# Two graph attention layers: own rows taken from gathered tiles, and the order of sums and turns in layer 1

## The chip, the cores and the metric

The kernel runs on one core of a Trainium2 chip. The metric is the device time of one execution in microseconds (us). The engines are PE (TensorE: matmuls, transposes), DVE (VectorE), ACT (ScalarE), POOL (GpSimd) and SP (SyncE, here only for DMAs). DMAs are issued by SP, ACT and POOL; the indirect ones, which gather or scatter rows by a list of row numbers, by POOL.

## The reference

There are 2708 nodes with 1024 features each, and an adjacency matrix in which a node has its own edge and about 16 others. Each layer is an attention over the neighbours, then a residual sum and a layer norm:

```python
def _L0_gnn_ref(x, adj, Wf, bf, Wg, bg, W, bW):
    e = jax.nn.relu((x @ Wf + bf) @ (x @ Wg + bg).T)
    scores = jnp.where(adj > 0, e, NEG)
    return jax.nn.softmax(scores, axis=1) @ (x @ W + bW)

def _L1_gnn_ref(x, adj, W, a1, a2):
    h = x @ W
    e = jax.nn.leaky_relu(h @ a1 + (h @ a2).T, negative_slope=0.2)
    scores = jnp.where(adj > 0, e, NEG)
    return jax.nn.relu(jax.nn.softmax(scores, axis=1) @ h)

x = _layernorm(x + _L0_gnn_ref(x, adj, ...), axis=-1)
x = _layernorm(x + _L1_gnn_ref(x, adj, ...), axis=-1)
```

## The kernel before

**Lists (lines 189 to 515).** In place of dense attention, the kernel turns each row of `adj` into a list of at most 40 neighbours. For each of 22 blocks of 128 rows, `lists(b)` (line 405) loads 128 x 2708 integers, makes them 0 or 1 on ACT with a row sum (410), multiplies them on POOL with `iota` (412), which holds 8192 minus the column, and takes the largest values on DVE: 8 from each of 20 segments (415), then 40 from those in five rounds (419). A larger value is a smaller column, so a list `L` holds its columns in rising order, with zeros behind the last. `keep_lists` (430) makes column numbers of it on ACT, 8192 for an unused place, and writes them to `LD` in device memory. These are ordered by the scheduler of the language. In between, PE forms `M = Wf Wg^T` and other small products, with copies on ACT and a few row operations on POOL (`row_parts`, 255). A node's number of neighbours gives its class; the nodes are sorted by class, and every 32 of the sorted nodes are a group: 85 groups with 3 to 10 tiles, 405 in all. Four groups are a block; block 0 has one group with 20 valid rows.

**A tile** is 128 gathered rows: partition 32q + i holds the neighbour at place 4t + q of the list of the group's node i, t being the tile's number in the group. So place 0 of all lists of a group lies in partitions 0 to 31 of its tile t = 0.

**Order of work.** From line 520 on all five engines are used through `InOrder` (line 61): instructions of one engine keep the order in which the program issues them. Each engine's queue is thus written by hand, and a waiting instruction holds up all behind it on its engine.

**Layer 0 (lines 868 to 1105)** gathers rows of `x` into a ring of 20 slots; per tile DVE forms 128 dot products (line 886), PE sums the rows with the softmax weights, turns the sums, and multiplies with `W`. `close(b)` (932) adds the residual, normalises, writes the rows to `X1S` by SP (948), forms two dot products (950, 951) and scatters the rows by POOL with their score to `T1`, from which layer 1 gathers.

**Layer 1 (lines 1108 to 1262).** `z = x1[done1[b] % 3]` names one of three buffers, `rb`, `u1b`, `u2b`. A ring of 33 slots (`ring` and `more`) holds gathered rows of `T1`, 4112 bytes each. The blocks run in the order of their sums of tiles. A block with four groups has two parts, `ks` = (0, 1) and (2, 3); block 0 has one; that makes 43 parts of 3 to 14 tiles. For each part the loop at line 1215 issues:

1. `lay.sums` (815): PE, two matmuls (both halves of the 1024 columns) per tile, into the bank `po`.
2. The rest of `closing`: POOL scatters a finished block to `out` (1171).
3. `lay.gathers(latest)` (669): POOL gathers into the slots that this part has freed, the slot freed last first.
4. One `piece` (1201), if one is there: the product of half a block with `M`, which now holds the layer's `W`, eight matmuls on PE.
5. `turn_half` (1207) of the part before: four transposes on PE; with a block's last part, its two halves are put into `pieces`.
6. `scores1` of the next part (1137): DVE adds and softmax weights, with one exponential on ACT (796).
7. `lay.out` (839): ACT writes `y`, the sums divided by their totals.
8. The copies of the turned part to `yT` on ACT.
9. After a block's last part, `mark_over` (1176) for two more blocks: POOL sets a mark in `over` for each tile that a group doesn't use, one memset per group; once, `count_over` (1185) compares the marks with the lists on DVE, PE and ACT.
10. If a block's second half product has just been issued, `close1` (1157): SP loads the block's rows of `X1S` into `z`, DVE adds relu of the product and computes mean and variance, ACT normalises.

Behind the loop the remaining half products and the last block follow (1249 to 1261).

The score of a gathered row lies at column 1024 of its slot. `unfit` (101, 1245) sends inputs that don't fit the lists to another path, which these inputs don't take.

Of the kernel before, what the change touches and what calls it, by code (L numbers as in the profile page):

```python
# [8 lines left out]
F32 = mybir.dt.float32  # L9
BF16 = mybir.dt.bfloat16  # L10
I32 = mybir.dt.int32
AF = mybir.ActivationFunctionType
ALU = mybir.AluOpType
# [22 lines left out]
NONE = 8192  # L36
# [21 lines left out]
TILES = [SORTED[_g] for _g in GROUPS]  # L58
# [48 lines left out]
def listed_path(ctx, tc, x, adj, Wf, bf, Wg, bg, W, bW, W1, a1, a2, out):  # L107

    nc = tc.nc
    P = 128  # L110
    N, D = x.shape
    KC = D // P
    H = D // 512
    TW = D + 4
    NB = (N + P - 1) // P
# [4 lines left out]
    valid = [N - 32 * (NG - 1)] + [P] * (NB - 1)  # L120
    start = [0] + [valid[0] + P * b for b in range(NB - 1)]
# [19 lines left out]

    LD = dram.tile([N * Q, QT], I32, name="LD")
    T1 = dram.tile([N, TW], F32, name="T1")
    X1S = dram.tile([N, D], F32, name="X1S")

    ident = const.tile([P, P], F32, name="ident")
    make_identity(nc, ident)
# [49 lines left out]
    with tc.tile_pool(name="pre", bufs=1) as pre:  # L197
# [8 lines left out]
        for t in (tot, cnt, cls):  # L206
            nc.vector.memset(t, -1.0)
        nc.vector.memset(L[:, NB - 1, :], 0.0)
        none = pre.tile([P, 1], F32, name="none")
        nc.gpsimd.memset(none, float(NONE))  # L210

        def ramp(name, count, step, base, dtype=F32, part=0):
            t = pre.tile([P, count], dtype, name=name)
            nc.gpsimd.iota(t, pattern=[[step, count]], base=base, channel_multiplier=part,
                           allow_small_or_imprecise_dtypes=True)
            return t

        fours = ramp("fours", QT, 4, 0)
        classes = ramp("classes", NCL, 1, 0)
        lows = ramp("lows", 32, 1, 0)  # L220
# [31 lines left out]
        with tc.tile_pool(name="adjp", bufs=3) as adjp, tc.tile_pool(name="cands", bufs=2) as cands, \  # L252
# [152 lines left out]
            def lists(b):  # L405
                n = nsize[b]
                t = adjp.tile([P, N], I32, name="adj")
                sp.dma_start(t[:n], adj[b * P:b * P + n, :])
                k = t.bitcast(F32)
                act.activation(k[:n], t[:n], AF.Relu, accum_out=tot[:n, b:b + 1])  # L410
                for cut in ([slice(0, 10 * SEG), slice(10 * SEG, N)] if b == 0 else [slice(0, N)]):
                    nc.gpsimd.tensor_tensor(k[:n, cut], k[:n, cut], iota[:n, cut], op=ALU.mult)  # L412
                cand = cands.tile([P, NSEG, 8], F32, name="cand")
                for s in range(NSEG):
                    nc.vector.max(cand[:n, s, :], k[:n, s * SEG:min((s + 1) * SEG, N)])  # L415
                flat = cand.rearrange("p s e -> p (s e)")
                for r in range(CAP // 8):
                    top = L[:n, b, r * 8:(r + 1) * 8]
                    nc.vector.max(top, flat[:n])
                    if r + 1 < CAP // 8:  # L420
                        nc.vector.match_replace(flat[:n], top, flat[:n], 0.0)
                j2 = cands.tile([P, CAP], F32, name="j2")
                nc.vector.tensor_scalar(j2[:n], L[:n, b, :], 0.0, 0.0, op0=ALU.is_gt, op1=ALU.add,
                                        accum_out=cnt[:n, b:b + 1])

                j3 = cands.tile([P, QT], F32, name="j3")
                nc.vector.tensor_scalar(j3[:n], fours[:n], cnt[:n, b:b + 1], 0.0, op0=ALU.is_lt, op1=ALU.add,
                                        accum_out=cls[:n, b:b + 1])

            def keep_lists(b):  # L430
                n = nsize[b]
                act.activation(PL[:n, b], L[:n, b].rearrange("p (t q) -> p q t", q=Q), AF.Relu,
                                     scale=-1.0, bias=none[:n])
                act.dma_start(LD.rearrange("(n q) t -> n (q t)", q=Q)[b * P:b * P + n, :],
                                    PL[:n, b].rearrange("p q t -> p (q t)"))

# [65 lines left out]
        for q in range(Q):  # L502
# [8 lines left out]
        t = pre.tile([P, NB], F32, name="badu")  # L511
        nc.vector.tensor_scalar(t, cnt, 0.0, 0.0, op0=ALU.is_equal, op1=ALU.add, accum_out=bad[:, 2:3])
        t = pre.tile([P, NB], F32, name="badv")
        nc.vector.tensor_scalar(t, L[:, :, 0], float(NONE), 0.0, op0=ALU.is_gt, op1=ALU.add,
                                accum_out=bad[:, 3:4])


# [351 lines left out]
    with ExitStack() as s0s:  # L869
# [62 lines left out]
        def close(b):  # L932

            n, m, z = nrows[b], valid[b], Z.pop(b)
            pm = Wp.pop(b)

            def add(h):
                c = slice(h * 512, (h + 1) * 512)
                dve.tensor_add(z[:n, c], pm[h][:n, h, :], z[:n, c])

            if b + 1 < NB:
                dve.tensor_add(z[:n, :D], flat(pm)[:n], z[:n, :D])
            steps = norm(z, n, None if b + 1 < NB else add)
            next(steps)
            yield
            for _ in steps:
                pass
            sp.dma_start(X1S[start[b]:start[b] + m, :], z[:m, :D])
            yield
            dot(z[:n, :D], u2b, n, z[:n, D:D + 1])  # L950
            dot(z[:n, :D], u1b, n, f1[:n, b:b + 1])
            yield
            if z is not zs:
                pool.memset(z[:, D + 1:], 0.0)
            scatter(T1[:, :], ids[:m, b:b + 1], z[:m])
# [152 lines left out]
    with ExitStack() as s1s:  # L1108
# [28 lines left out]
        def scores1(u, ks):  # L1137
# [16 lines left out]
            dve.tensor_add(sc, sc, off)  # L1154
            lay.soft(u, ks)

        def close1(b, pm):
            m, z = valid[b], x1[done1[b] % 3]
            sp.dma_start(z[:m], X1S[start[b]:start[b] + m, :])
            last = b == order1[-1]  # L1160

            def add(h):
                c = slice(h * 512, (h + 1) * 512)
                dve.scalar_tensor_tensor(z[:m, c], pm[h][:m, h, :], 0.0, z[:m, c], op0=ALU.max, op1=ALU.add)

            if not last:
                dve.scalar_tensor_tensor(z[:m], flat(pm)[:m], 0.0, z[:m], op0=ALU.max, op1=ALU.add)
            for _ in norm(z, m, add if last else None):
                pass
            yield  # L1170
            scatter(out, ids[:m, b:b + 1], z[:m])
# [4 lines left out]
        def mark_over(b):  # L1176

            for g in groups[b]:
                if g == 0:
                    for q in range(Q):  # L1180
                        pool.memset(over[32 * q:32 * q + valid[0], 0, TILES[0]:], 1.0)
                elif TILES[g] < QT:
                    pool.memset(over[:, g, TILES[g]:], 1.0)

        def count_over():
            dve.scalar_tensor_tensor(over, SL, float(N), over, op0=ALU.is_lt, op1=ALU.mult)
# [5 lines left out]

        parts = [(u, ks) for u in units for ks in (((0, 1), (2, 3)) if u.G == Q else ((0,),))]
        lay.gathers()
        pool.memset(over, 0.0)
        scores1(*parts[0])
        closing, pieces, turning = iter(()), [], None
        banks = ps_s.tile([P, H, 512], F32, name="po")
        yT = {}

        def piece(b, h, pm):
            if h == 0:
                pm.append(ps_m.tile([P, H, 512], F32, name="pm"))
            half_product(pm[0], h, nrows[b], yT[b], M)
            return (b, pm[0]) if h + 1 == H else None

        def turn_half(u, ks, y):
            b = u.b
            if ks[0] == 0:
                yT[b] = tp.tile([P, KC, P], F32, name="yT")  # L1210
            steps = lay.turn(y, ks, yT[b])
            next(steps)
            return steps

        for n, (u, ks) in enumerate(parts):
            b, po = u.b, banks[:, n % 2, :]
            latest = lay.sums(u, po, ks)
            for _ in closing:
                pass
            closing = iter(())  # L1220
            lay.gathers(latest)
            made = pieces.pop(0)() if pieces else None
            steps = iter(())
            if turning is not None:
                v, kv, _ = turning
                steps = turn_half(*turning)
                if kv[-1] + 1 == v.G:
                    pm = []
                    pieces += [lambda c=v.b, h=h, pm=pm: piece(c, h, pm) for h in range(H)]
            if n + 1 < len(parts):  # L1230
                scores1(*parts[n + 1])
            y = yp.tile([P, 512], F32, name="y1")
            lay.out(u, po, ks, y)
            for _ in steps:
                pass
            turning = u, ks, y
            if ks[-1] + 1 == u.G:
                k = done1[b]
                for i in (2 * k, 2 * k + 1):
                    if i < NB:  # L1240
                        mark_over(i)
                if k == NB // 2 + 1:
                    count_over()
                if k + 2 == NB:
                    unfit = nc.values_load(flag[0:1, 0:1])
            if made is not None:
                closing = close1(*made)
                next(closing)
        while pieces:
            made = pieces.pop(0)()  # L1250
        for _ in turn_half(*turning):
            pass
        for _ in closing:
            pass
        closing = close1(*made)
        next(closing)
        prod = two_products(P, yT[b], M)
        for _ in closing:
            pass
# [366 lines left out]
```

## Time and profile before

| | |
|---|---|
| median of 3 executions | 1890.39 us (1887.95 to 1898.44) |
| the profiled execution | 1750.29 us, span 1748.6 us |
| mean clock granted to PE | 0.957 |
| busy: PE, DVE, ACT, POOL | 1563.6, 1297.5, 643.5, 1180.9 us |
| moved by DMA | 502.8 MB, mean 288 GB/s |
| read from and written to device memory | 509.6 MB, 33.8 MB |
| gathers in layer 0, layer 1 | 405, 249 + 156 |
| transfers of `X1S`: written, read | 22, 22 (512 KB each for a full block) |

The span is the time from the first to the last instruction of the profiled execution. In views by time, columns are the start and the length in us, the engine, the line, the operation and the tiles that it writes and reads; a bracket behind gives the idle time of the engine just before, and what ended it. Since nearly all engine calls of the two layers pass through `InOrder`, they carry its line, L71; the names of the tiles tell them apart: `po` are the weighted sums, `pm` the products, `pt` the turned data. `ring<-in_x_dram,SL` is a gather of layer 0, `ring<-T,SL` and `more<-T,SL` are gathers of layer 1. "issue" is time in which an engine waited for nothing that the profile shows.

### The profile page before, as it was taken

How to read it: one execution, taken by the hardware profiler on the slowest of the kernel's cores; microseconds unless marked ns; L12 is line 12 of the kernel's file. 1: busy time of each engine (PE TensorE's matmuls, PEld its weight loads, DVE VectorE, ACT ScalarE, POOL GpSimd, SP SyncE). 2: the span in 40 equal slices, each digit the busy share in tenths (PEclk: the TensorE clock that was granted, in tenths of full speed). 3: DMA queues.
4: the chain of work that ended last, by engine and by line, in shares of the span. 5: the costliest groups of instructions: out<-in, count | busy, mean ns of one | idle time of the engine just before them, and what ended most of it. 6: DMA issues, size and time to landing. Idle time of an engine off the chain costs nothing. (4 is left out here: it accounts for less than half of the span.)

```text
span 1748.6 us, 23112 instructions
## 1 busy us (share of the span) xinstructions
PE 1563.6 (89%) x6969; PEld 675.5 (39%) x6969; DVE 1297.5 (74%) x4262; ACT 643.5 (37%) x902; POOL 1180.9 (68%) x1195
## 2 busy tenths in 40 slices
PE   4999578899999999999999999559899888999896
PEld 2444233344444444444444444213344333343332
DVE  5879846899999989998999977547465555665652
ACT  4555455444444554555554444101111111111111
POOL 7888476467667767776677743177777777777740
PEclk8999778999999999999999999879999999999998
DMA  7656168578877777888887876399999999999960
GB/s 287 228 185 236 38 232 309 199 252 292 302 277 283 269 253 276 294 293 284 303 299 285 291 267 249 121 394 357 367 374 392 391 397 375 384 392 390 396 253 38
DMA packets 149986, 502.80 MB, mean 288 GB/s; under 512 B 32340, under 2 KB 32372, under 8 KB 147144
## 3 DMA queue, kind: packets, MB, share of 16 engines
q0 software_dynamic: 132032, 428.29, 66.2%
q1 hardware_dynamic: 10202, 55.72, 8.4%
q10 hardware_dynamic: 7618, 17.23, 2.7%
q8 instruction: 57, 0.93, 0.2%
q14 instruction: 77, 0.63, 0.1%
HBM read 509.64 MB, written 33.75 MB: 311 GB/s over the span
## 5 line engine op out<-in xcount | busy, mean ns | idle before, releaser
L71 POOL DMA_INDIRECT ring<-in_x_dram,SL x405 | 429.9, 1062 | 164.0 <-issue 70.0
L71 DVE SCALAR_TENSOR_TENSOR j<-ring,Fr 128x1024 bf16<-128x1024 f32 x402 | 493.9, 1229 | 41.1 <-DMA ring<-in_x_dram,SL 13.9
L71 PE MATMUL po<-ring,st 128*32 128x512 f32 x2616 | 324.4, 616 | 56.9 <-ACT y L71 32.5
L71 ACT COPY Fr<-pm 32x1024 f32<-32x1024 f32 (+2 forms) x353 | 340.6, 965 | 18.8 <-PE pm L71 14.1
L71 PE MATMUL pm<-M,yT 128*128 128x512 f32 (+1 forms) x704 | 313.3, 598 | 0.5 <-ACT yT L71 0.5
L71 PE MATMUL pm<-Wt,xT 128*128 128x512 f32 (+1 forms) x704 | 300.5, 599 | 4.7 <-DMA Wt<-in_L_gnn_W_dram 4.7
L71 POOL DMA_INDIRECT ring<-T,SL x249 | 247.0, 992 | 80.5 <-issue 66.3
L71 PE MATMUL pm<-M,xT 128*128 128x512 f32 x672 | 297.5, 601 | 0.0
L71 ACT ACTIVATE scores<-scores 128x12 f32<-128x12 f32 (+9 forms) x65 | 14.0, 216 | 631.6 <-DVE scores L71 631.6
L71 PEld LDWEIGHTS pm<-M,yT 128*128 128x128 f32 (+1 forms) x704 | 127.8, 186 | 185.0 <-issue 183.8
L71 PEld LDWEIGHTS pm<-Wt,xT 128*128 128x128 f32 (+1 forms) x704 | 131.0, 189 | 163.4 <-issue 154.6
L71 PEld LDWEIGHTS pm<-M,xT 128*128 128x128 f32 x672 | 130.2, 194 | 158.0 <-issue 155.1
L71 POOL DMA_INDIRECT more<-T,SL x156 | 154.6, 991 | 48.5 <-issue 43.8
L71 PEld LDWEIGHTS po<-ring,st 128*32 128x32 f32 x2616 | 95.9, 113 | 229.8 <-issue 174.0
L412 POOL TENSOR_TENSOR adj<-adj,iota 128x2708 f32<-128x2708 f32 (+3 forms) x23 | 130.6, 5685 | 22.7 <-ACT adj L71 22.6
L415 DVE MAX8 cand<-adj 128x8 f32<-128x136 f32 (+2 forms) x440 | 97.2, 285 | 37.4 <-POOL adj L412 37.4
L71 PE MATMUL pm<-halfT,WfT 128*128 128x512 f32 x256 | 114.1, 601 | 1.1 <-ACT WfT L71 1.1
L71 POOL DMA_INDIRECT SL<-LD,idq x85 | 86.4, 1016 | 25.8 <-issue 24.0
L71 PE MATMUL po<-more,st 128*32 128x512 f32 x624 | 82.4, 625 | 14.3 <-ACT y L71 14.3
L71 DVE TENSOR_SCALAR scores<-ring,f1q 128x4 f32<-128x4 f32 (+6 forms) x69 | 16.5, 245 | 104.1 <-DMA ring<-T,SL 93.1
L71 POOL DMA_INDIRECT z<-in_x_dram,ids x21 | 24.0, 1142 | 87.1 <-DVE j L71 36.4
L71 PEld LDWEIGHTS pm<-halfT,WfT 128*128 128x128 f32 x256 | 48.2, 193 | 58.0 <-issue 55.2
(214 smaller groups left out, 1539.5 us busy)
## 6 DMA issues: line engine op xcount, KB each, us to landing
adj<-in_adj_dram SPq DMA_DIRECT2D x21, 1354.0 KB, 5.8
X1S<-z SPq DMA_DIRECT2D x19, 512.0 KB, 5.2
ring<-in_x_dram,SL POOLq DMA_INDIRECT x405, 6.5
rows<-in_L_gnn_Wg_dram ACTq DMA_DIRECT2D x8, 512.0 KB, 4.4
rows<-in_L_gnn_Wf_dram ACTq DMA_DIRECT2D x8, 512.0 KB, 3.5
rows<-in_L_gnn_W_dram ACTq DMA_DIRECT2D x8, 512.0 KB, 6.1
Wt<-in_L_gnn_W_dram ACTq DMA_DIRECT2D x1, 4096.0 KB
M<-in_L_gnn_W_dram SPq DMA_DIRECT2D x1, 4096.0 KB
```

The source lines that it names most:

```text
L71: made = self.tc.keep_in_program_order(op(*args, **kwargs))
L412: nc.gpsimd.tensor_tensor(k[:n, cut], k[:n, cut], iota[:n, cut], op=ALU.mult)
L415: nc.vector.max(cand[:n, s, :], k[:n, s * SEG:min((s + 1) * SEG, N)])
```

## The change

The own key of each row is doubled on POOL, so that it is the largest of its list and comes to place 0; ACT halves it again when the column numbers are made. The rows of `X1S` are then the rows 0 to 31 of the tiles with t = 0, which layer 1 gathers in any case. `X1S` goes, with its writes in layer 0 and its loads in layer 1. `own_rows` copies the rows from the ring to `z` on ACT, one copy of 32 x 1024 per group, behind the copies of the turned part in the loop. `y` and the turning now belong to the same part: `lay.out` is issued ahead of the half product, `turn_half` behind it, and the scores of the next part after both. The half products of a block so start one part earlier, and the steps behind the loop that finished the last turn and one half product go. `mark_over` and the clearing of `over` are issued on DVE. The test on the first place of a list compares the other way.

```diff
-    X1S = dram.tile([N, D], F32, name="X1S")
...
+        nc.vector.memset(L[:, NB - 1, 0:1], 4.0 * NONE)
...
+        twice = SL.rearrange("p g t -> p (g t)").bitcast(F32)[:, :P]
+        nc.gpsimd.tensor_scalar(twice, ident, 1.0, None, op0=ALU.add)
...
+                own = slice(b * P, b * P + n)
+                nc.gpsimd.tensor_tensor(k[:n, own], k[:n, own], twice[:n, :n], op=ALU.mult)
...
+                act.activation(PL[:n, b, 0, 0:1], L[:n, b, 0:1], AF.Relu, scale=-0.5, bias=none[:n])
...
-        nc.vector.tensor_scalar(t, L[:, :, 0], float(NONE), 0.0, op0=ALU.is_gt, op1=ALU.add,
+        nc.vector.tensor_scalar(t, L[:, :, 0], float(NONE), 0.0, op0=ALU.is_le, op1=ALU.add,
...
-            sp.dma_start(X1S[start[b]:start[b] + m, :], z[:m, :D])
...
+        def own_rows(u, ks):
+
+            z = x1[done1[u.b] % 3]
+            for k in ks:
+                m = next(i for i, tile in enumerate(u.tiles) if tile[0] == k)
+                n = min(32, valid[u.b])
+                act.copy(z[32 * k:32 * k + n], lay.rows(u.at + m)[:n, :D])
+
         def close1(b, pm):
             m, z = valid[b], x1[done1[b] % 3]
-            sp.dma_start(z[:m], X1S[start[b]:start[b] + m, :])
...
-                        pool.memset(over[32 * q:32 * q + valid[0], 0, TILES[0]:], 1.0)
+                        dve.memset(over[32 * q:32 * q + valid[0], 0, TILES[0]:], 1.0)
                 elif TILES[g] < QT:
-                    pool.memset(over[:, g, TILES[g]:], 1.0)
+                    dve.memset(over[:, g, TILES[g]:], 1.0)
...
-        pool.memset(over, 0.0)
+        dve.memset(over, 0.0)
         scores1(*parts[0])
-        closing, pieces, turning = iter(()), [], None
+        own_rows(*parts[0])
+        closing, pieces = iter(()), []
...
             lay.gathers(latest)
+            y = yp.tile([P, 512], F32, name="y1")
+            lay.out(u, po, ks, y)
             made = pieces.pop(0)() if pieces else None
-            steps = iter(())
-            if turning is not None:
-                v, kv, _ = turning
-                steps = turn_half(*turning)
-                if kv[-1] + 1 == v.G:
-                    pm = []
-                    pieces += [lambda c=v.b, h=h, pm=pm: piece(c, h, pm) for h in range(H)]
+            steps = turn_half(u, ks, y)
+            if ks[-1] + 1 == u.G:
+                pm = []
+                pieces += [lambda c=b, h=h, pm=pm: piece(c, h, pm) for h in range(H)]
             if n + 1 < len(parts):
                 scores1(*parts[n + 1])
-            y = yp.tile([P, 512], F32, name="y1")
-            lay.out(u, po, ks, y)
             for _ in steps:
                 pass
-            turning = u, ks, y
+            if n + 1 < len(parts):
+                own_rows(*parts[n + 1])
...
-        while pieces:
-            made = pieces.pop(0)()
-        for _ in turn_half(*turning):
-            pass
-        for _ in closing:
-            pass
-        closing = close1(*made)
-        next(closing)
         prod = two_products(P, yT[b], M)
```

## The prediction, made before the result was known

> **What bounds the kernel now.** I read three views in this order: the busy tenths of the whole span (page, part 2), the busy times by stage over layer 1, and the order in time of single engines where layer 1 begins, runs and ends.
>
> ```profile
> PE   4999578899999999999999999559899888999896
> DVE  5879846899999989998999977547465555665652
> POOL 7888476467667767776677743177777777777740
> DMA  7656168578877777888887876399999999999960
> ```
>
> Slices are 43.7 us. Slices 1 to 5 make the lists, up to slice 25 is layer 0 (PE and DVE full, POOL and DMA not), slices 27 to 39 are layer 1. There the DMA engines stand at 9, PE near 9 and POOL at a steady 7. The steady 7 is the important one:
>
> ```profile
> 1300.00:1400.00 100.00, 90.67 (x441) 39.82 (x439) 58.77 (x286) 14.75 (x34) 77.29 (x101) 0.98 1.01 388
> 1500.00:1600.00 100.00, 96.12 (x470) 39.85 (x463) 59.18 (x282) 14.89 (x32) 76.53 (x78) 0.98 1.01 391
> ```
>
> Columns: PE, PE loads, DVE, ACT, POOL busy, clock, DMA share, GB/s. Looked at instruction by instruction, POOL's 77 is a full queue:
>
> ```profile
> 1219.91 0.99 POOL L71 DMA_INDIRECT more<-T,SL  x1 [0.30 <-issue]
> 1221.20 0.99 POOL L71 DMA_INDIRECT more<-T,SL  x1 [0.30 <-issue]
> 1222.18 0.37 POOL L71 MEMSET over<- 128x3 f32 x8
> 1222.70 1.00 POOL L71 DMA_INDIRECT ring<-T,SL  x1 [0.15 <-issue]
> ...
> 1664.44 1.01 POOL L71 DMA_INDIRECT ring<-T,SL  x1 [0.30 <-issue]
> 1667.46 0.99 POOL L71 DMA_INDIRECT more<-T,SL  x1 [2.02 <-issue]
> ```
>
> Each gather occupies POOL for 0.99 + 0.30 = 1.295 us, back to back. From the first gather at 1133.72 to the last at 1686.89, 553.2 us, there are 404 steps: 404 x 1.295 = 523.2, 18 scatters of `out` x 1.31 = 23.6, and what is left, 6.4 us, is memsets and a few stalls. The same 1.295 stands at the start, when the DMA engines have just become busy, and the waits of POOL between 1200 and 1640 are almost only "issue" of 0.3. So layer 1 is paced by POOL's issuing, with the DMA engines (share 1.0) and PE close behind: a block of 20 tiles costs POOL 20 x 1.295 + 1.5 = 27.4 us and PE 24.2 (sums 5.45 + 3.64, two half products of 7.13, two turns of 0.43).
>
> After the last gather PE sets the end:
>
> ```profile
> 1700.56 4.03 PE L71 MATMUL po<-ring,st 128*32 128x512 f32 x34
> 1704.52 7.13 PE L71 MATMUL pm<-M,yT 128*128 128x512 f32 x16
> 1711.49 0.60 PE L71 MATMUL pt<-ident,y 128*128 128x128 f32 x4
> 1711.92 7.03 PE L71 MATMUL pm<-M,yT 128*128 128x512 f32 x16
> 1718.79 0.60 PE L71 MATMUL pt<-ident,y 128*128 128x128 f32 x4
> 1719.86 14.00 PE L71 MATMUL pm<-M,yT 128*128 128x512 f32 x32 [0.46 <-ACT yT L71]
> ```
>
> Last sums, a half product, a turn, the block's other half product, the last turn, the last block's product: two half products lie between the last sums and the last product.
>
> [...] gathers landed 6.2 us after issue at the start of layer 1 (1136.37 to 1142.56) and up to 10.3 later, beside reloads of X1S and scatters. [...] the trace has 5.94 us for 2708, 2.19 ns. [...] the trace's scaled pass over 128x1024 in SBUF is 1.24, its 32x1024 copies out of PSUM 1.0. [...] here the clock is 0.97 to 1.0 wherever PE is busy.
>
> **The change part by part.**
>
> *X1S is no longer written (22 SP transfers).* These lie in layer 0, where PE (97%) and DVE (92%) are full and DMA is at 0.67 to 0.84. DVE waited 13 us for gathers in all of it. I take 0; bounds -3 and 0.
>
> *X1S is no longer read (22 transfers, 11.1 MB).* At 388 GB/s this is 28.6 us of DMA time, but POOL's pace doesn't follow from DMA time. Three places do. (a) At the seam:
>
> ```profile
> 1127.05 1.33 POOL L71 DMA_INDIRECT T<-ring,ids  x1 [14.05 <-DVE j L71]
> 1133.72 1.03 POOL L71 DMA_INDIRECT ring<-T,SL  x1 [5.33 <-DMA T<-ring,ids]
> ```
>
> The first gather waits for the last scatter, 5.87 us, with three 512 KB transfers of X1S and one of 80 KB started from 1125.0 to 1128.8. The DMA view has a median of 3.7 for the two scatters of this kind, and 3.4 for the fastest of all. I take -2.2 (bounds -2.5, 0). (b) The gather at 1667.46 stalled 1.7 us beyond 0.3, three before it 0.3 together, where landings took 10 us. I take half of 2.0: -1.0 (-2.0, 0). (c) Landing of the last but one part, whose last gather went out at 1675.23 and whose scores were complete at 1683.1: 7.9 us against 6.2 undisturbed. I take -0.8 (-1.7, 0).
>
> *Own rows on ACT: 85 copies at 1.1 us* [...], 2.2 us per part. ACT is busy 15 of 100 us in layer 1, so I take 0. The wait counts more: the first copies of a block overwrite the buffer whose `out` scatter belongs to three blocks before. Behind them on ACT stand the normalised rows of another block, the next `y`, then the next exponential, for which PE and DVE wait. Putting each scatter just ahead of the gathers that follow it in the new order, and 7.5 us for its landing, it lands 11 and 9 us after ACT asks for it in two early blocks, and from 2.8 late to 4.2 early in the others. About 9 us of lateness are covered (3.6 to 5.4 of sums and 7.1 of half product on PE, less ACT's own 3). So PE loses some 2 us early, where POOL is 18 to 20 us behind the slots that PE has freed: hidden. Without that cover it would be 2 us.
>
> *Sums turned at once.* Per part nothing is added. On ACT the exponential now follows `y`; `y` waits for the sums just ended and has the half product (7.1) as cover. One half product moves from the tail into the second part of layer 1, where PE waited 3.4 us for data, so PE runs some 3.5 us later from there; slots are freed at least 5.3 us ahead of the gather that takes them, so POOL doesn't see it. In the tail one of the two half products and a turn gap go: 1704.52 to 1719.86 is 15.3, afterwards 7.1 + 0.43 + 0.5: **-7.3** (-8, -5). One more scatter (1.31 us) stands before the last 7 gathers; the last part's sums waited for PE and not for data (exponential at 1694.5, sums at 1700.1), so 0.
>
> *Marks on VectorE.* On POOL go: the clearing (1176.27 to the next gather 0.98, less 0.30), the first eight marks (1.39 less 0.30) and ten groups of eight at 0.22 beyond the usual gap, as at 1222.18: 0.7 + 1.1 + 2.1 = **-3.9** (-4.2, -3). On DVE eight memsets at 0.08 per block, 0.7 us, where it is busy 59%; the clearing falls into its wait of 13 us for the first gather: 0.
>
> *Own key first.* Per block POOL gets a 128x128 product: 128 x 2.19 = 0.28, with a gap 0.34. It counts where DVE waits for POOL:
>
> ```profile
> 136.10 0.30 DVE L415 MAX8 cand<-adj 128x8 f32<-128x136 f32 x1 [1.69 <-POOL adj L412]
> 197.85 1.30 DVE L415 MAX8 cand<-adj 20x8 f32<-20x136 f32 x6 [0.26 <-POOL adj L412]
> ```
>
> Up to 136.1 POOL runs from 111.72 with three blocks: 3 x 0.34. From there DVE works without a gap to 197.85, where POOL is again just in time, with two more on its side: 5 x 0.34 = **+1.7** (+1, +2.8). `twice` (about 0.3) is under POOL's wait of 0.5 for the first mask. A one-column ACT pass per block (0.16 to 0.2) is under ACT's waits of 3.6 us per step for PE. Comparing the other way costs nothing.
>
> **Sum:** -2.2 - 1.0 - 0.8 - 7.3 - 3.9 + 1.7 = **-13.5**, so the profiled execution of 1750.3 (span 1748.6) becomes 1736.8, a ratio of 0.9923. The shown runs have a median of 1890.4, 140 us more, and the profile doesn't say where those lie; I carry the ratio over: 1875.9, written **1876**.
>
> **The rivals.**
> *PE paces the runs.* If the 140 us are slower matmuls, PE's 24.2 us per block reach POOL's 27.4, and what POOL saves is worth nothing; a half product that only moves saves the 3.4 us of early idle less 2 for ACT's wait. With -2.2 + 1.7 this is about -2: 1888. For it: PE is near full in both layers. Against it: the clock in the trace [...].
> *DMA time paces the runs.* If the 140 us are slower transfers, the bytes count: -28.6 - 2.2 - 7.3 + 1.7 = -36, 1851. For it: share 1.0. Against it: 1.295 at any load.
> *The copies stall ACT (slower).* If scatters land later than I place them, for instance 13 us after ACT's need in all 19 full blocks, PE loses 13 - 9 = 4 per block, 3.2 of them within POOL's margin; at 15 us it is 2.8 beyond the margin, 19 x 2.8 = 53 less 13.5 gained: about 1930; it turns into a loss against the present from 12.9. For it: the two early blocks. Against it: in the rest the order in time leaves it near 0.
> *An unseen wait at the gathers* (85 of them now also follow an ACT copy) at a sixth of the 0.30 gap each, a guess, gives back 4: 1880.
>
> **How the numbers follow.** Forecast 0.47, with the unseen wait 0.1; PE 0.22; DMA 0.1; ACT stall or another loss 0.11. Within the forecast its bounds give 1869 to 1883. 0.5% (9.5 us, about what a measurement of this kernel can tell from no change) puts the line at 1881. Faster: 0.43 of the forecast, 0.06, and DMA's 0.1, less a little: 0.57; within 0.5%: 0.31; slower 0.12. The range takes in PE's case and half of DMA's: 1859 to 1892.
>
> **What would show it.** Right: no transfer of X1S; POOL from first to last gather 548 us or less, still at 1.295; one half product between the last sums and the last product; first gather 2 us sooner after the last scatter; lists ending 1 to 3 us later. Wrong: ACT copies with idle time released by `out`; POOL waiting for PE or ACT; a gather step other than 1.295 with DMA below 1.

## The result, and the profile after

The changed kernel took **1956.13 us** (median of 4 executions, 1947.51 to 1960.44), against 1891.87 for the kernel before in the same set of runs (4 executions, 1887.95 to 1898.44): a ratio of **1.0387** (95% interval 1.0326 to 1.0448). Forecast were 1876 and 0.9923. The change made this measurement slower by 3.9%.

The same program differed by up to 9% between sets of runs: the kernel before had medians of 1892, 1903, 1897 and 1905 us in four sets and of 1748, 1749 and 1750 in three. So all ratios here are within one set. They leave out executions that stand more than 1.5% above the fastest of their kernel; where I count executions, all of them are counted.

The page of the changed kernel, 40 slices of 49 us. Added to the rows that were shown of before is the clock granted to PE:

```profile
PE   5999468688888889899999989469978887978886
DVE  5979447778767777688888868426635454555543
POOL 8988444555555555566676752366664666666640
PEclk9999679788888989899999999769988998999988
DMA  6745346656666666667777775399886999999960
```

Layer 0 is slices 5 to 26. In slices 9 to 16 (counted from 1) DVE has fallen from 8 or 9 to between 6 and 8, POOL from 6 or 7 to 5, DMA from 7 or 8 to 6 (5 in one), and the clock stands at 7 to 9. After that the slices of layer 0 come back towards those of before. The stretch in numbers, and two stretches of layer 1 (columns as in the windows of before: PE, PE loads, DVE, ACT, POOL busy, clock, DMA share, GB/s):

```profile
430.00:880.00 450.00, 398.15 (x1665) 169.54 (x1665) 338.16 (x753) 190.87 (x228) 254.74 (x244) 0.90 0.63 222
880.00:1090.00 210.00, 201.41 (x902) 89.14 (x901) 184.56 (x407) 103.78 (x125) 145.06 (x134) 1.00 0.76 261
1300.00:1400.00 100.00, 92.29 (x404) 32.94 (x406) 57.74 (x320) 31.62 (x51) 65.28 (x67) 0.92 0.89 311
1500.00:1600.00 100.00, 86.53 (x376) 33.84 (x380) 49.93 (x255) 27.09 (x43) 62.28 (x63) 0.90 0.86 307
```

The first row has 1665 matmuls in 450 us at a mean clock of 0.90. In layer 1 POOL has fallen from 77 to between 62 and 65, with DMA below 0.9: POOL's queue no longer paces it. An instant from layer 1 shows what does (all engines in order of time):

```profile
1705.04 1.03 PE L71 MATMUL po<-ring,st 128*32 128x512 f32 x4
...
1705.99 7.13 PE L71 MATMUL pm<-M,yT 128*128 128x512 f32 x16
...
1706.73 0.17 DVE L71 TENSOR_TENSOR scores<-scores,mq 128x10 f32<-128x10 f32 x1
...
1716.16 0.69 ACT L71 ACTIVATE y<-po,ri 128x512 f32<-128x512 f32 x1 [11.77 <-remote]
1716.34 0.99 POOL L71 DMA_INDIRECT ring<-T,SL  x1 [2.03 <-remote]
1716.74 0.20 ACT L71 ACTIVATE scores<-scores 128x10 f32<-128x10 f32 x1
...
1716.90 0.33 PE L71 MATMUL pt<-ident,y 128*128 128x128 f32 x1 [3.77 <-issue]
```

The sums of a part end at 1706.1 by the page's model. `y` on ACT, which needs them, starts 10 us later, and in the same moment POOL gets the slots that these sums have freed. "remote" and "issue" say that the page has no releaser. In the trace's own record of PE's semaphore the step of these sums comes at 1716.09, 0.07 us ahead of `y`, and that of the half product behind them, modelled end 1713.13, at 1716.24. I call this **late ends**, and the opposite, steps at the modelled ends, prompt ends. The exponential (`scores<-scores`) is issued behind `y` on ACT and starts at 1716.74, 9.8 us after DVE finished its input (1706.90): a waiting instruction held up the one behind it.

Late ends are not the change's doing: a new profile of the unchanged kernel before (first experiment) has them too, and then takes 1914 us. The profile of before that I predicted from has none, and took 1750. Its timed runs and its profile were not of one kind. In layer 1 of the control POOL stood idle before its gathers for 75 us beyond the usual 0.3 each, and 73 of these end within 0.45 us of a step of PE's semaphore; in the profile of before that was shown it was 2 us, and none so. So with late ends POOL waits for slots that PE frees. By stage, from the traces (us; the lists end where DVE starts its last removal of values; layer 0 ends with the last scatter to `T1`; half clock is the time in which the trace shows PE's clock at 0.5, in layer 1 from its first gather on):

| kernel, span | lists end | layer 0 | to first `T` gather | first to last gather | to the end | half clock in layer 0, 1 |
|---|---|---|---|---|---|---|
| before, shown, 1748.6 | 204.7 | 922.4 | 6.7 | 553.2 | 61.7 | 62, 65 |
| before, control, 1914.3 | 202.1 | 1004.2 | 6.8 | 627.3 | 73.9 | 106, 114 |
| changed, result, 1958.7 | 204.9 | **1050.1** | 4.5 | 632.5 | 66.7 | **183**, 139 |
| changed, third set, 1717.2 | 204.5 | 909.4 | 4.5 | 548.5 | 50.2 | 46, 53 |
| changed, fourth set, 1962.2 | 205.7 | **1029.3** | 4.5 | 656.4 | 66.2 | **152**, 153 |
| changed, fifth set, 1905.0 | 205.4 | 987.2 | 4.5 | 640.2 | 67.7 | 86, 131 |

Against the control, layer 1 of the result's profile is not longer: 699 us against 701 from its first gather. Its 46 us more are in layer 0, whose blocks 2 to 10 (counted from 0, from one scatter to `T1` to the next) took 45 to 54 us each with 7 to 13 us of half clock in each, and the next six 41 to 43 us.

### The profile page after: what moved, and what is told of

Read it like the earlier page. It is cut to its first block, busy times and chain, and to the rows that moved or that the text cites. A ratio compares the mean times of both kernels' runs of the same rounds, so it can differ in the third digit from the quotient of the medians.

```text
span 1958.7 us, 23156 instructions
## 1 busy us (share of the span) xinstructions
PE 1662.0 (85%) x6969; PEld 698.6 (36%) x6969; DVE 1295.9 (66%) x4351; ACT 740.2 (38%) x1009; POOL 1187.0 (61%) x1130
## 5 line engine op out<-in xcount | busy, mean ns | idle before, releaser
L71 DVE SCALAR_TENSOR_TENSOR j<-ring,Fr 128x1024 bf16<-128x1024 f32 x402 | 494.2, 1229 | 90.5 <-issue 37.3
L71 PE MATMUL po<-ring,st 128*32 128x512 f32 x2616 | 350.2, 626 | 40.8 <-issue 28.7
L71 PE MATMUL pm<-Wt,xT 128*128 128x512 f32 (+1 forms) x704 | 313.2, 609 | 36.7 <-issue 36.7
L71 PE MATMUL pm<-M,yT 128*128 128x512 f32 (+1 forms) x704 | 322.6, 606 | 17.4 <-issue 16.1
L71 PE MATMUL pm<-M,xT 128*128 128x512 f32 x672 | 321.3, 636 | 11.2 <-issue 11.2
L71 PEld LDWEIGHTS pm<-M,xT 128*128 128x128 f32 x672 | 138.6, 206 | 188.4 <-issue 186.2
L71 DVE TENSOR_TENSOR st<-scores,stack 128x128 f32<-128x128 f32 (+9 forms) x122 | 41.2, 377 | 223.6 <-ACT scores L71 201.3
L71 PEld LDWEIGHTS po<-ring,st 128*32 128x32 f32 x2616 | 104.5, 114 | 227.4 <-issue 202.7
L71 ACT ACTIVATE y<-po,ri 128x512 f32<-128x512 f32 (+1 forms) x88 | 58.0, 684 | 270.3 <-remote 128.7
L71 ACT COPY xT<-pt 128x512 f32<-128x512 f32 (+2 forms) x109 | 48.6, 498 | 181.5 <-PE pt L71 111.3
L71 POOL DMA_INDIRECT SL<-LD,idq x85 | 87.0, 1024 | 25.8 <-issue 23.6
L71 PE MATMUL po<-more,st 128*32 128x512 f32 x624 | 95.7, 681 | 6.1 <-issue 6.1
```

What stands on the lines that cost most here:

```text
L71: made = self.tc.keep_in_program_order(op(*args, **kwargs))
```

## The experiments

They were sent in six sets. Each ratio is against the kernel before in its own set.

### First set (before 1902.85 us, 57 executions)

My first theory, A, was the order in layer 1: with late ends, `y` comes late, and in the new order the exponential stands behind it on ACT. The rival B was the own rows or the lists. The control has no edit.

> The kernel before, unchanged, as a control. The profile shown of it had a span of 1748.6 us, 140 us under its timed runs; the profile of the changed kernel (span 1958.7) agrees with its timed runs and shows PE finishing later than its matmuls' modelled ends from 245 us on (weighted sums reported done 4 to 10 us late in layer 1), also in layer 0 where nothing was changed. Theory A (the loss is the order: y, and behind it the exponential, wait for sums that are reported late): this run is at 1890 us with a mean clock near 0.92 and the same late ends in its trace, and its parts don't wait for them. Theory B (the loss is the own-row copies on ACT or the lists): same time, and nothing can be said of late ends. Ratio 1.00 in both.

Measured: 0.9991 (0.9948 to 1.0034), clock 0.938, with late ends: between 1300 and 1700 us, of 68 matmuls that step PE's semaphore only 22 have a step within 0.2 us of their modelled end (in the profile shown of before 81 of 81).

The order alone, in the kernel before:

```diff
+            y = yp.tile([P, 512], F32, name="y1")
+            lay.out(u, po, ks, y)
             made = pieces.pop(0)() if pieces else None
-            ...turn_half(*turning)...
+            steps = turn_half(u, ks, y)
```

> The kernel before with the new order of sums, y and turn alone (X1S, lists and marks as before). Theory A: nearly the whole loss, ratio 1.03 to 1.04 (1950 to 1965 us). Theory B: the shorter tail alone, ratio 0.995 to 1.00.

Measured: **0.9996** (0.9945 to 1.0047). Theory A's loss of 3 to 4% isn't there.

The changed kernel with the old order:

```diff
-    R0, R1 = 20, 33
+    R0, R1 = 20, 32
-        x1 = [rb, u1b, u2b]
+        x1 = [rb, u1b, u2b, ovp.tile([P, D], F32, name="z4")]
...the loop and its tail as before, own_rows behind lay.out...
```

> The changed kernel with the loop's order put back (a part is turned one part later, the exponential ahead of y); own rows, own key and marks stay. A fourth z buffer is needed then, and the ring has 32 slots instead of 33 to make room for it. Theory A: the loss is gone, ratio 0.99 to 1.005. Theory B: the loss stays, ratio 1.03 to 1.04.

Measured: 1.008 (1.0037 to 1.0123). B's 3 to 4% isn't there either; the 0.8% may come from the smaller ring, which wasn't tried alone.

The changed kernel with the exponential first:

```diff
+            if n + 1 < len(parts):
+                scores1(*parts[n + 1])
             y = yp.tile([P, 512], F32, name="y1")
             lay.out(u, po, ks, y)
...
-            if n + 1 < len(parts):
-                scores1(*parts[n + 1])
```

> The changed kernel with the scores of the next part issued ahead of y, so that on ACT the exponential no longer stands behind y; the part is still turned at once. Theory A with the exponential as the link that costs: most of the loss goes, ratio 0.99 to 1.015. Theory A with the turn as the link (PE's transposes wait for y): ratio stays above 1.02. Theory B: stays at 1.03 to 1.04.

Measured: **0.995** (0.991 to 0.9991). Its layer 0 is that of the changed kernel and took 971.6 us, with 64 us of half clock. With these three runs neither A nor B explains the result, and the long layer 0 doesn't come with this code in every condition. That made theory C: the loss is clock that wasn't granted in layer 0.

### Second set (before 1748.06 us, 19 executions)

The changed kernel, no edit:

> The changed kernel, unchanged, once more. Its first profile lost its time in layer 0: 1050 us from the end of the lists to the last scatter of T1, with PE's clock at half for 183 us of them, against 1004 and 107 in the control; its layer 1, from the first gather to the end, took 699 us against 701. Layer 0 is the same code in two of the experiments that took 971 and 994 there. Theory C (the loss is clock that was not granted in layer 0, and no part of the edit takes it): here the ratio is 0.99 to 1.01, layer 0 takes 970 to 1010 us with 60 to 110 us at half clock. Theory A (the order costs what the exponential waits for) or B (own rows, lists): ratio 1.03 to 1.045 again.

Measured: **0.9856** (0.9835 to 0.9877), 1722.85 us. No late ends here (in layer 1, between 1200 and 1600 us, all steps within 0.2 us).

No `X1S`, in the kernel before:

```diff
-            sp.dma_start(X1S[start[b]:start[b] + m, :], z[:m, :D])
...
-            sp.dma_start(z[:m], X1S[start[b]:start[b] + m, :])
```

> The kernel before without its 22 writes and 22 loads of X1S; the residual of layer 1 is left out with them. If the DMA engines' time paces layer 1: 28 us less, ratio 0.985. If POOL's issuing or PE paces it: the seam and little more, ratio 0.995 to 1.00.

Measured: 0.9915 (0.9894 to 0.9935), so 15 us less; DMA time's 28 isn't reached. Layer 0 took 913.9 instead of 918.6 to 922.4 in three profiles with the writes.

Less work for PE, in the kernel before:

```diff
-            half_product(pm[0], h, nrows[b], yT[b], M)
+            for k in range(KC - 1):
+                pe.matmul(..., start=(k == 0), stop=(k == KC - 2))
```

> The kernel before with seven of the eight matmuls in each half product of the loop of layer 1; an eighth of the features is left out of the product. It takes 42 x 0.88 = 37 us of PE's work out of layer 1 and nothing from any other engine. If PE paces layer 1 in the timed runs: 25 to 37 us less, ratio 0.98 to 0.987. If POOL's issuing paces it: the tail's 2 us, ratio 0.998.

Measured: 0.9989 (0.9973 to 1.0004). With prompt ends 37 us less on PE bring about 2: POOL's issuing paces layer 1 there, as the prediction had it. This wasn't tried with late ends.

### Third set (before 1748.98 us, 12 executions)

> The changed kernel once more. So far: 1.0387 against runs of before at 1892 us, and 0.986 on a chip where before takes 1748 us and PE's ends are prompt in the trace. If before takes about 1900 us here (late ends). Theory A (with late ends, y and behind it the exponential come late in every part): ratio 1.02 to 1.045, and layer 1 longer than in the two kernels beside it. Theory C (the loss was clock that was not granted, in layer 0, by the conditions of those runs): 0.985 to 1.00. If before takes about 1748 us: 0.986 again, and nothing is told apart.

Measured: **0.9841** (0.9817 to 0.9865). The stretches of layer 0 and 1 of this run:

```profile
430.00:880.00 450.00, 440.73 (x2019) 191.60 (x2018) 417.73 (x922) 228.49 (x275) 313.65 (x302) 1.00 0.79 279
...
1500.00:1600.00 100.00, 90.91 (x462) 41.24 (x464) 61.57 (x293) 31.99 (x50) 76.54 (x78) 1.00 0.99 375
```

2019 matmuls where the result's profile had 1665, and POOL back at 76.5. The counterpart of the instant shown above:

```profile
1493.57 1.03 PE L71 MATMUL po<-ring,st 128*32 128x512 f32 x4
...
1494.53 0.70 PE L71 MATMUL pm<-M,yT 128*128 128x512 f32 x1
1494.69 0.69 ACT L71 ACTIVATE y<-po,ri 128x512 f32<-128x512 f32 x1 [1.71 <-issue]
```

`y` starts 0.1 us after the sums' modelled end (1494.60), with the half product as cover.

> The changed kernel with the next part's scores issued ahead of y. With before at 1900 us it had 0.995. With before at 1748 us: Theory A says that the order of y and exponential doesn't matter where ends are prompt (the half product covers y): the ratio of the changed kernel within 0.003. A rival says that y behind the exponential delays the turn: 0.99 to 0.995.

Measured: 0.986 (0.9834 to 0.9886), the changed kernel's ratio within 0.002. With prompt ends it makes no difference that could be measured which of `y` and the exponential stands first.

> The kernel before with the new order of sums, y and turn alone. With before at 1900 us it had 1.000. With before at 1748 us the shorter tail shows, 7 to 12 us: ratio 0.993 to 0.996.

Measured: 0.9941 (0.992 to 0.9963), 11 us less; the stretch after the last gather is 50.8 us instead of 61.7. By the numbers that they carry, this set and the fifth ran on the same chip.

### Fourth set (before 1897.37 us, 27 executions, 1869 to 1918)

> The changed kernel once more, for a chip on which before takes about 1900 us. In its first profile the first ten blocks of layer 0 took 49 to 56 us each with 7 to 15 us of PE's clock at half in each, and 43 us after that; its blocks of layer 1 took 30.7 us, as those of the control (30.9). Theory C (these ten blocks are the whole loss, and the edit doesn't bring them): with before at 1900 us the ratio is 0.985 to 1.0, the blocks of layer 0 take 43 us from the second or third on. Theory C2 (the edit brings them: without the writes of X1S layer 0 runs into the half clock): ratio 1.02 to 1.045, ten blocks near 50 us. Theory A: ratio 1.02 to 1.045, blocks of layer 1 longer than 31 us. With before at 1748 us: 0.985.

Measured: **1.023** (1.0163 to 1.0298), 1934 to 1972 us in 6 executions, medians 1956.9 against 1897.4. The changed kernel is slower again, and all six of its executions are longer than all 27 of before: blocks 2 to 8 of layer 0 took 48 to 51 us with 8 to 13 us of half clock each, then 42 to 43.

> The kernel before without writes and loads of X1S (the residual of layer 1 left out), once more. With before at 1748 us it had 0.9915, 8.5 us of it in layer 0. With before at about 1900 us: Theory C2: blocks near 50 us in layer 0 as in the changed kernel's first profile, ratio above 1.02. Theory C: 0.985 to 1.0.

Measured: 0.9997 (0.9956 to 1.0039). But of all its 20 executions 7 took 1946 to 1986 us at a mean clock of 0.910 to 0.919, and 13 took 1878 to 1930 at 0.927 to 0.944. Of the 27 of before beside it none took more than 1918, at 0.930 to 0.945. The profile is of one of the 13 (layer 0: 979.6 us, with one block of 52.4 us and 7 us of half clock among blocks of 41 to 44). So in this set leaving out `X1S` alone went with long executions, in a third of the cases; the whole change had them in 6 of 6. The line between long and short isn't sharp: the shortest of these six took 1934 us at a clock of 0.929, the longest of the 13 took 1930 at 0.927. By the numbers that the chips carry, no other set ran on this set's chip; the result's chip isn't recorded.

### Fifth set (before 1904.72 us, 58 executions)

`X1S` is written again in the changed kernel:

```diff
+    X1S = dram.tile([N, D], F32, name="X1S")
...
+            sp.dma_start(X1S[start[b]:start[b] + m, :], z[:m, :D])
```

> The changed kernel with the writes of X1S put back in layer 0; nothing reads them. Theory C2 (without the writes layer 0 runs into the half clock) with before at about 1900 us: blocks of 43 us in layer 0, ratio 0.985 to 1.005. If another part of the edit brings it: ratio 1.02 to 1.045 as in the changed kernel beside it. With before at 1748 us: the writes give back most of the 8.5 us that layer 0 gained, ratio 0.989 to 0.992.

Measured: 0.9953 (0.9927 to 0.9978). From the third on its blocks took 41 to 44 us, but for two of 47 and 46 us with 5 and 3 us of half clock.

> The changed kernel beside it. With before at about 1900 us 1.02 to 1.045 by Theory C2; by the theory that only the moment of the first measurement counts, 0.985 to 1.0. With before at 1748 us: 0.985.

Measured: **0.9997** (0.997 to 1.0024), 1887 to 1913 us in 22 executions, clock 0.935 to 0.946. The blocks of layer 0 take 41 to 44 us from the second on, up to the short ones at its end:

```profile
430.00:880.00 450.00, 435.00 (x1945) 191.92 (x1954) 392.63 (x885) 218.76 (x264) 310.27 (x284) 1.00 0.76 258
...
1500.00:1600.00 100.00, 85.05 (x373) 32.07 (x371) 48.08 (x251) 25.52 (x42) 66.40 (x68) 0.94 0.91 324
```

The same program in the same stretch as in the result's profile: 1945 matmuls instead of 1665, the clock at 1.00 instead of 0.90. Layer 1 looks as it did there. The difference lies in layer 0: it is 62.9 us shorter, with 97 us less of half clock (by an estimate worth at most half of it, 48 us, since in the result's profile the products' matmuls come 0.43 us apart at a clock of 1.0 and 0.85 at 0.5). PE is busy for 435 us of the 450 here, and was for 398 there.

> The changed kernel with the exponential ahead of y; its layer 0 is that of the changed kernel. Before at about 1900 us: by Theory C2 the same as the changed kernel within 0.01 (it had 0.995 on a chip where the changed kernel wasn't run); if layer 1's order is what costs: 0.995 again, and 0.03 under the changed kernel. Before at 1748 us: 0.986.

Measured: 0.9959 (0.9924 to 0.9995). It lies 0.004 under the changed kernel, as in size the late exponential would make it, but the intervals overlap.

### Sixth set (before 1749.83 us, 11 executions)

It was meant for the condition of the fourth set, and came in that of the third.

> The changed kernel once more, as the control of the two beside it. In conditions like those of the first measurement 1.02 to 1.045 with blocks of 50 us in layer 0; otherwise 1.000 with before at 1900 us, 0.985 with before at 1748 us.

Measured: 0.9842 (0.9816 to 0.9868).

> The changed kernel with the writes of X1S in layer 0. If the changed kernel beside it has the blocks of 50 us and the missing writes bring them: 0.99 to 1.005 here. If another part or the condition alone brings them: as the changed kernel within 0.01. With before at 1900 us and no such blocks: 0.995 again; with before at 1748 us: 0.989 to 0.992.

Measured: 0.988 (0.9862 to 0.9899): the writes cost 2.8 us between the medians (1727.74 and 1724.93).

> The changed kernel with the exponential ahead of y; layer 0 is the changed kernel's. If the changed kernel has the blocks of 50 us: this one too, within 0.01 of it. With before at 1900 us and no such blocks: 0.004 under the changed kernel again (0.995 to 0.996), from layer 1; with before at 1748 us: 0.986.

Measured: 0.9858 (0.9838 to 0.9877). Whether the writes keep the long blocks away where these occur was thus not measured.

## Why the prediction was wrong

**The step that failed** is the last of the sum: "the profile doesn't say where those lie; I carry the ratio over". The 140 us between the profile and the timed runs belong to another condition of the machine, with other bounds. The control, against the profile shown, is 82 us longer in layer 0 and 86 from layer 1's first gather on, with late ends and 93 us more at half clock. In the measurement that was forecast, the changed kernel's layer 0 then took 46 us more than that of the control, which ran in the first set, in a stage where the prediction had taken 0. In the condition of the profile the forecast's sign was right and its size half of what came (-25, -30 and -25 us in three sets). With late ends the change is worth nothing that could be measured (0.9997), and in the sets with long blocks in layer 0 it loses 2 to 4%.

With it fell what the prediction held against the rival that PE paces the runs, a clock that stays up. That the timed runs had it was my estimate and not shown. The traces here have clocks of 1.0 and 0.5 only, and in the result's profile PE stood at half clock for 183 us of layer 0. Nor was the clock 0.97 to 1.0 wherever PE is busy: in the profile I read, it was 0.74 from 1687 to 1692 us with PE busy all through, and PE stood at half for 62 us of layer 0.

By its steps, in the condition of its own profile:

- *POOL's issuing paces layer 1, 1.295 us per gather*: right. First to last gather 548.5 us in the third set (548 or less was asked), the step is still 1.295, and PE's work is worth next to nothing (0.9989). With late ends it is wrong: POOL gets its slots late (58 to 69 busy of 100), and a full block takes about 31 us in the control and in the changed kernel alike, instead of 27.2.
- *X1S no longer written: 0*: wrong by the profiles. Six profiles without the writes have 909.4 to 917.0 us in layer 0, four with them 918.0 to 922.4; the means differ by 7.6, the timed pair of the sixth set by 2.8. I put 3 us as the bound because DVE waited only 13 us for gathers. But these waits were partly the writes' own doing. The waits of DVE and PE from 350 to 1050 us, in the kernel before:

```profile
DVE j L71 <- DMA ring<-in_x_dram,SL: 12.0, 22, 1.2
```

```profile
PE po L71 <- DVE st L71: 5.4, 9, 1.0
```

and in the changed kernel of the third set:

```profile
DVE j L71 <- DMA ring<-in_x_dram,SL: 2.2, 4, 1.0
```

```profile
PE po L71 <- DVE st L71: 0.8, 2, 0.5
```

  The columns are us in total, times, longest. DVE's dot products wait 10 us less for gathered rows, and PE 4.6 us less for the weights that follow from them. In the sixth set, where the writes alone are put back, these waits are 8.4 against 3.9 and 3.8 against 0.8.
- *Seam -2.2*: right. POOL's last scatter and first gather:

```profile
1113.97 1.34 POOL L71 DMA_INDIRECT T<-ring,ids  x1 [16.14 <-DVE j L71]
1118.50 1.03 POOL L71 DMA_INDIRECT ring<-T,SL  x1 [3.19 <-DMA T<-ring,ids]
```

  4.5 us instead of 6.7. With the writes alone put back it is still 4.6 to 4.7, so the loads had made it long.
- *Marks -3.9 and POOL's late stall -1.0, with a scatter of 1.3 more*: nearly right: -3.6 together, and -4.7 measured between first and last gather.
- *Tail -7.3 and landing -0.8*: -11.5. PE's end, to be held against the lines of before:

```profile
1663.87 4.72 PE L71 MATMUL po<-more,st 128*32 128x512 f32 x40 [1.30 <-DVE st L71]
...
1676.49 4.03 PE L71 MATMUL po<-ring,st 128*32 128x512 f32 x34
1680.45 7.13 PE L71 MATMUL pm<-M,yT 128*128 128x512 f32 x16
1687.42 0.60 PE L71 MATMUL pt<-ident,y 128*128 128x128 f32 x4
1688.48 14.00 PE L71 MATMUL pm<-M,yT 128*128 128x512 f32 x32 [0.46 <-ACT yT L71]
```

  One half product and one turn are gone: from the last sums to the end 37.3 us instead of 44.6, the -7.3. The term that was too small is the one ahead of it. The last sums start their last matmul 12.9 us after the last gather instead of 17.1: 4.2 us, where I had 0.8 for landing. The sums of the last part but one, the first line, start 3.2 us ahead of the last gather and take 4.7 us; in the profile of before they started 0.2 us ahead (1686.68) and took 6.0, with PE's clock at 0.74. So 1.3 us are clock and 2.9 an earlier start. Of these, most is the order: with the new order alone and `X1S` still read, they start 2.5 us ahead. There, too, a scatter of 1.3 us stands ahead of the last gathers, so that these come later and part of the gain is only moved from one stretch to the other. Leaving out `X1S` alone gives 1.3 ahead, 1.1 more than before: landing was sized about right.
- *Lists +1.7*: 0, and why wasn't pursued. POOL's 128x128 product takes 0.46 us in the result's profile (21 of them), where I had 0.28 from the time per element of the 128x2708 one (5.94 us). With prompt ends the lists end at 203.2 to 205.2 with the own key and at 204.5 to 205.4 without.
- *Own rows on ACT: 0, with 2.2 us per part*: right; the 1.1 us per copy were an estimate, and two copies take 2.11. In the third set ACT waited 7.1 us in all for `out` scatters ahead of them. The rival of the stall (1930) is out.
- *Per part nothing is added*: right with prompt ends (0.9841 and 0.986). With late ends the cover of 7.1 us isn't one, as the instant at 1716 shows; the fifth set has 0.004 for it, which is within the noise there.

Added up: 0 - 7.6 - 2.1 - 4.7 - 11.5 = -25.9, against -25 to -30 measured. What the forecast's -13.5 lacked are 7.6 of the writes, 3.4 behind the last gather, and the 1.7 of the lists that didn't come.

**Where the 3.9% come from.** The time lies in some ten blocks of layer 0, where PE's clock is at half for about 10 us of 50 in each; the same program without these blocks is at 0.9997. But the half clock isn't what comes first in them. One such block in the result's profile, PE alone, and then its windows around the moment at which the clock falls (424.8; columns as above):

```profile
409.66 11.32 PE L71 MATMUL pm<-Wt,xT 128*128 128x512 f32 x26
422.41 0.59 PE L71 MATMUL pm<-Wt,xT 128*128 128x512 f32 x1 [1.43 <-issue]
424.50 0.73 PE L71 MATMUL pm<-Wt,xT 128*128 128x512 f32 x1 [1.50 <-issue]
...
421.00:424.80 3.80, 0.89 (x2) 0.37 (x2) 3.73 (x6) 0.00 (x0) 2.95 (x3) 1.00 0.82 245
424.80:435.00 10.20, 7.21 (x11) 2.78 (x11) 4.78 (x9) 4.61 (x5) 4.96 (x5) 0.50 0.75 254
```

The product has 32 matmuls; the first 26 come 0.43 us apart, and then, still at a clock of 1.00, they come up to 2.1 us apart, for no reason that the page shows. The fifth set's profile has all 32 in 13.9 us. In each of the 16 stretches at half clock in these blocks (nine in the result's profile, seven in the fourth set's) such gaps begin 2.8 to 5.6 us before the clock falls. Over blocks 2 to 10 the result's profile is 67 us longer than the fifth set's, and 41 of these are more gaps between matmuls; the rest is slower matmuls at most. Of the gaps, 27 us lie ahead of the moments at which the clock falls, so theory C, clock that wasn't granted, can't be the whole loss. Whether PE stood idle in the gaps or was late with matmuls already recorded, the trace doesn't tell.

What the missing writes have to do with it is not shown. For a link: in the fourth set, without `X1S` alone, executions of that length and clock come in 7 of 20, and in none of the 27 of before beside them. Against a firm one: time and clock alone don't prove these blocks (in the fifth set one execution of the kernel before took 1940 us at 0.931, another 1933 at 0.937); milder ones, of 46 and 47 us, stand in the profile with the writes kept; and 75 executions of three kernels without the writes (22, 39 and 14, in the first and fifth sets) took 1871 to 1923 us. That matmuls which stand closer together bring the half clock is not borne out: the third set's profile has 2019 of them in the 450 us where the result's has 1665, and no half clock there. The changed kernel with the writes put back never met the condition, which two of the seven measurements met, the first included. What the condition is, a chip or a moment, why the matmuls come apart in it, and whether the rest of the change adds to it (6 of 6 against 7 of 20) stay open.

None of the rivals was this. "PE paces the runs" (1888, a ratio of 0.999) fits the fifth set by its size alone; with late ends no run took work from PE, so its mechanism wasn't tried there.

## What to carry to other kernels

If a profile's own time and the timed runs differ by more than the runs among themselves (here 1750 us against 1888 to 1898), they come from different conditions: find what differs (clock by stage, and the distance from a matmul's end to what waits for it) before a ratio is carried over, or give a forecast for each. Where a stretch has both a low clock and idle time, see which of them begins first (here the gaps, by 2.8 to 5.6 us) before the clock is called the cause. A wait that is small in the profile can be the very cost of the transfer that goes (in the sixth set DVE's dot products waited 8.4 us for gathered rows with the writes and 3.9 without); it bounds nothing from above unless something else is known to cause it. And repeat a surprising ratio in other sets: here the same two programs gave 0.984, 1.000, 1.023 and 1.039.

## What the hardware showed that I had not expected

- One program, one core, by its number also one chip: 1749 us in one set and 1905 in another.
- Late ends: with them, PE's semaphore steps for two groups of matmuls 7 us apart came 0.16 us apart (1716.085 and 1716.244). Their cause isn't known, and neither is whether PE is late or only its signal.
- PE's clock was granted at 1.0 or 0.5 in pieces of 3.4 us, nothing between. In the result's profile, stretches of about 10 us at half came about once per block of layer 0 from 363 to 834 us, then no more until 1152. In the long blocks they follow gaps between matmuls, which begin 2.8 to 5.6 us earlier. In line with this, the kernel before with less work for PE in layer 1 stood at half for 95 us there, with prompt ends, against 64 to 66 in three kernels with the full work and 53 in the changed kernel of the third set.
